# Convolution and input projection of a four-layer selective scan: from 128 output columns at once to pairs of 64

## The chip, the cores and the metric

The kernel runs on one core of one Trainium2 chip. The metric is the device time of one launch in microseconds; lower is better. A state in this text is one of the 16 state channels of the scan, and "128*64" in a row of the profile is a matmul with 128 rows of contraction and 64 output columns (output partitions).

## What is computed

Four layers are applied to x of 8 x 48 x 48 x 96, each as `x = x + ss2d(groupnorm(x))`. Cut to what matters, one layer is:

```
xz = x @ in_proj_w.T;  xc, z = split(xz)               # 192 channels each
xc = silu(depthwise_conv3x3(xc) + conv_b)              # over 48 x 48
for each of 4 directions k (rows, columns, both reversed):
    dt, B, C = split(x_proj[k] @ xc)                   # rank 6 or 16, 16, 16
    delta = softplus(dt_proj[k] @ dt + bias)
    h[n] = exp(delta*A[n]) * h[n] + delta*xc*B[n]      # a scan of 2304 steps, n = 0..15
    y += sum_n h[n]*C[n] + D*xc
out = out_proj @ (layernorm(y) * silu(z))
```

The last layer replaces the recurrence by a form with cumulative sums, of which the kernel computes 192 positions at each end and tests that the others have faded.

## The kernel before

Channels lie on partitions. Batches go in pairs, so a layer has four pairs, and the 192 channels of two batches make three tiles of 128 (t = 0 and 1 are the first 128 channels of one batch each, t = 2 the last 64 of both). In layers 0 to 2 the scan goes over 12 groups a pair (tile, phase, direction), each in three chunks of 768 positions, each chunk over 16 states: 4 x 3 x 12 x 3 x 16 = 6912 states in all.

One state takes these steps. SyncE fetches a row of C into `cb` and for 6 of 16 states a row of B into `bb` (`fetch`, L718). For the other 10, TensorE spreads B over the partitions into the PSUM tile `b` (`spread_rows`, L667, bf16, 96*64). ScalarE computes the decay `da` (L764), VectorE multiplies `b` by `du` (L794) and scans (L798), GpSimd multiplies by `bb` (L741) and by `cb` (L807), and TensorE adds pairs of states up into `acc` by the stationary matrix `twin` (`add_up`, L854, f32, 128*64 with 384 columns moving, a pair of halves). `prepare` makes the step sizes of the next chunk: L603, ScalarE's functions (L611 to L617), L623 (sums of four terms, again in pairs of 64 columns, both halves reading the same rows), copies to `dl` and `du` (L578).

The rest of a layer is written as generators whose steps go beside the scan. `prologue` of the next pair loads x, normalises it, projects it (L404 for the first 128 channels, L413 for the last 64, in row blocks of 480 or 384 positions) into the padded images `pad` and `pad2`, and convolves (`convolve`): for each of three tiles and five row blocks, nine matmuls L312 with diagonal stationary matrices `diag` add up in one PSUM bank, and ScalarE evicts them (L320). Then come the projections of x (L465) and the conversion of B to three bf16 parts. `epilogue` of the pair before does the layer norm (L1012 to L1018), the gate (L1074, L1078) and the output (L1092 to L1098, in the last layer L1113 to L1115).

```
            def beside():
                step(coming)

                for _ in range(10 if l in short else 0 if ends else 1):
                    side_step(rest) or side_step(behind, ahead)
```

So in layers 0 to 2 at most one side step goes with a state, and one matmul of the convolution is one step. In the last layer up to ten steps go with four states of the short form (class `Edge`, L930 to L995), and the convolution's matmuls stand in runs. PSUM banks for all of this are taken in turn from `psum` with two buffers (`bank()`).

For layers 0 to 2 `keep_order` holds every engine to the order in which the code issues instructions; the start and the last layer are ordered by the scheduler of the layer below.

Of the kernel before, what the change touches and what calls it, by code (L numbers as in the profile page):

```python
# [49 lines left out]
P = 128  # L50
NB, H, W, DM = 8, 48, 48, 96
# [52 lines left out]
def ss2d_layers_kernel(ctx: ExitStack, tc: tile.TileContext, x_in, consts, weights, out):  # L104
    nc = tc.nc
# [162 lines left out]
    def silu(o, i, **kw):  # L268

        with tc.issue_after(nc.scalar.activation(o, i, AF.Silu, **kw).ins):  # L270
            nc.scalar.preload_act_table_set("natural_log_exp_and_others")

    def bank():
        return psum.tile([P, BANK], F32, name="ps", tag="ps")
# [8 lines left out]


    GATED, READY = "gated", "ready"

    def prologue(l, p, short=False, first=False):
        ly = layers[l]
# [7 lines left out]
        def padded(name):  # L296
            pad = tmp.tile([P, H + 2, W + 2], F32, name=name, tag="tmp")
            nc.gpsimd.memset(pad[:, 0 : H + 2 : H + 1, :], 0.0)
            nc.gpsimd.memset(pad[:, 1 : H + 1, 0 : W + 2 : W + 1], 0.0)
            return pad  # L300

        def convolve(pad, t):

            while place["tiles"] < t and not first:
                yield GATED
            u[t] = upool.tile([P, L], F32, name=f"u_{l}_{p}_{t}", tag="u")
            for c0, m in CHUNKS:
                r0, nr = c0 // W, m // W
                ps = bank()
                for j in range(9):  # L310
                    dy, dx = divmod(j, 3)
                    nc.tensor.matmul(  # L312
                        ps[:, :m],
                        ly.diag[:, int(t == 2), j, :],
                        pad[:, r0 + dy : r0 + dy + nr, dx : dx + W],
                        start=(j == 0),
                        stop=(j == 8),
                    )
                    yield True
                nc.scalar.activation(  # L320
                    u[t][:, c0 : c0 + m], ps[:, :m], AF.Identity, bias=ly.column(t, C_CONVB)
                )
                yield
            silu(u[t], u[t])
            yield
# [6 lines left out]
        for b in range(2):  # L332
            x = tmp.tile([DM, L], F32, name=f"x_{l}_{p}_{b}", tag="tmp")
            if l == 0:
                loaded = []

                def load(c0, m):
                    ld = sm2.tile([P, 4, DM], F32, name="ld", tag="ld")
                    nc.sync.dma_start(
                        ld[: m // 4],  # L340
                        x_in[2 * p + b, c0 : c0 + m, :].rearrange("(q j) c -> q j c", j=4),
                    )
                    loaded.append(ld)

                load(*CHUNKS[0])
                load(*CHUNKS[1])
                for _ in range(3):
                    yield
                for i, (c0, m) in enumerate(CHUNKS):
                    q, ld = m // 4, loaded[i]  # L350
                    ps = bank()
                    for j in range(4):
                        nc.tensor.transpose(
                            ps[0:DM, j * q : (j + 1) * q], ld[:q, j, :], ident[:q, :q]
                        )
                    yield True
                    nc.scalar.copy(
                        x[:, c0 : c0 + m].rearrange("c (q j) -> c j q", j=4),
                        ps[0:DM, :m].rearrange("c (j q) -> c j q", j=4),
                    )  # L360
                    if i + 2 < NCH:
                        load(*CHUNKS[i + 2])
                    yield
                nc.sync.dma_start(src[b], x)
            else:
                nc.sync.dma_start(x, src[b])
            for _ in range(4):
                yield


            st = sm1.tile([DM, NCH, 6], F32, name="st", tag="st")
            for i, (c0, m) in enumerate(CHUNKS):
                nc.vector.bn_stats(st[:, i, :], x[:, c0 : c0 + m])
                if i % 2 == 1:
                    yield
            mv = sm1.tile([DM, 2], F32, name="mv", tag="mv")
            nc.vector.bn_aggr(mv, st.rearrange("p a b -> p (a b)"))
            yield
            ps = bank()
            nc.tensor.matmul(ps[0:DM, 0:1], minus_group, mv[:, 0:1], start=True, stop=True)  # L380
            yield True
            mg = sm1.tile([DM, 1], F32, name="mg", tag="mg")
            nc.scalar.copy(mg, ps[0:DM, 0:1])
            dv = sm1.tile([DM, 1], F32, name="dv", tag="dv")
            nc.scalar.activation(dv, mv[:, 0:1], AF.Square, bias=mg)
            nc.scalar.activation(dv, dv, AF.Identity, bias=mv[:, 1:2])
            yield
            ps = bank()
            nc.tensor.matmul(ps[0:DM, 0:1], group_w, dv, start=True, stop=True)
            yield True  # L390
            scale, shift = gn[:, b, 0:1], gn[:, b, 1:2]
            nc.scalar.activation(scale, ps[0:DM, 0:1], AF.Ln, bias=gn_eps[0:DM])
            nc.scalar.activation(scale, scale, AF.Exp, scale=-0.5)
            nc.scalar.activation(shift, mg, AF.Copy, scale=scale)
            nc.scalar.activation(x, x, AF.Identity, bias=shift, scale=scale)
            yield

            pad = padded(f"pad_{l}_{p}_{b}")
            q0 = 64 * b
            for c0, m in CHUNKS:  # L400
                r0, nr = c0 // W, m // W
                rows = slice(1 + r0, 1 + r0 + nr)
                ps = bank()
                nc.tensor.matmul(  # L404
                    ps[:, :m], ly.inw[:, 0:P], x[:, c0 : c0 + m], start=True, stop=True
                )
                yield True
                nc.scalar.copy(
                    pad[:, rows, 1 : W + 1], ps[:, :m].rearrange("p (r w) -> p r w", w=W)
                )  # L410
                yield
                ps = bank()
                nc.tensor.matmul(  # L413
                    ps[q0 : q0 + 64, :m], ly.inw[:, P:DIN], x[:, c0 : c0 + m], start=True, stop=True
                )
                yield True
                nc.scalar.copy(
                    pad2[q0 : q0 + 64, rows, 1 : W + 1],
                    ps[q0 : q0 + 64, :m].rearrange("p (r w) -> p r w", w=W),
                )  # L420
                yield
            if not (first and b == 1):
                yield from convolve(pad, b)
        yield from convolve(pad2, 2)


# [124 lines left out]
        if first:  # L551

            yield from x_projections((0, 0))
            yield READY
            yield from x_projections((1, 0))
            yield from convolve(pad, 1)
            yield from x_projections((0, 1), (1, 1))
        else:
            yield from x_projections((0, 0), (0, 1), (1, 0), (1, 1))
# [610 lines left out]
    def run(pairs, short):  # L1170
# [16 lines left out]
        def begin(l, p, first=False):  # L1187
            if l not in layers:
                layers[l] = Layer(l)
            return prologue(l, p, l in short, first)  # L1190
# [110 lines left out]
    ps = bank()  # L1301
# [100 lines left out]
```

## Time and profile before

| | |
|---|---|
| median of 3 runs | 20514.42 us (20494.02 to 20516.52) |
| profiled execution | 20509.65 us, its span 20507.7 us |
| mean granted TensorE clock | 0.904 |
| L312 matmul records, busy | 4320 (two for each of 2160 f32 matmuls), 2165.7 us |
| L404 matmul records | 320 |
| layers 0 to 2, from the first state to the last | 204 to 18564 us |
| last layer with its epilogues | 18564 to 20508 us |

The profile is of one execution. PE is TensorE's matmuls, PEld its weight loads, DVE VectorE, ACT ScalarE, POOL GpSimd, SP SyncE. Starts of matmuls are recorded and their ends are modelled, so the text takes the time from one start to the next where it says how long a matmul holds TensorE. A row of a group gives its count, then busy time and mean duration in ns, then the idle time ahead of it and what ended that. A row of the waits gives the total in us, the number of waits and the longest. `clock` is the share of full speed that TensorE was granted.

### The profile page before, as it was taken

How to read it: one execution, taken by the hardware profiler on the slowest of the kernel's cores; microseconds unless marked ns; L12 is line 12 of the kernel's file. 1: busy time of each engine (PE TensorE's matmuls, PEld its weight loads, DVE VectorE, ACT ScalarE, POOL GpSimd, SP SyncE). 2: the span in 40 equal slices, each digit the busy share in tenths (PEclk: the TensorE clock that was granted, in tenths of full speed). 3: DMA queues.
4: the chain of work that ended last, by engine and by line, in shares of the span. 5: the costliest groups of instructions: out<-in, count | busy, mean ns of one | idle time of the engine just before them, and what ended most of it. 6: DMA issues, size and time to landing. Idle time of an engine off the chain costs nothing. (4 is left out here: it accounts for less than half of the span.)

```text
span 20507.7 us, 304889 instructions
## 1 busy us (share of the span) xinstructions
PE 17283.2 (84%) x88322; PEld 7546.6 (37%) x88322; DVE 17656.0 (86%) x14161; ACT 16243.7 (79%) x30020; POOL 17768.2 (87%) x10121
## 2 busy tenths in 40 slices
PE   8888888888888888888888888888888888888886
PEld 2323333333333333333333333333333333335565
DVE  5999999999999999999999999989989989995543
ACT  5777887887887887887877887877877877877776
POOL 5999999999999999999999999999999999995432
PEclk8998998998998999998998999988988998999997
DMA  5888888888888888888888888888888888883221
GB/s 147 223 221 222 219 220 224 222 219 221 220 225 222 219 229 221 221 229 219 221 228 220 217 225 219 218 218 220 217 219 219 220 219 222 219 220 109 76 72 51
DMA packets 1963444, 4200.13 MB, mean 205 GB/s; under 512 B 369456, under 2 KB 720048, under 8 KB 1948592
## 3 DMA queue, kind: packets, MB, share of 16 engines
q1 hardware_dynamic: 1961776, 4180.52, 77.8%
q8 instruction: 726, 11.89, 0.3%
q14 instruction: 942, 7.72, 0.2%
HBM read 4026.64 MB, written 152.27 MB: 204 GB/s over the span
## 5 line engine op out<-in xcount | busy, mean ns | idle before, releaser
L807 POOL TENSOR_TENSOR cb<-cb,da 128x768 f32<-128x768 f32 x4320 | 7831.3, 1817 | 799.5 <-issue 258.3
L854 PE MATMUL acc<-cb,twin 128*64 128x384 f32 x27648 | 7018.1, 542 | 663.6 <-POOL cb L807 660.3
L798 DVE TENSOR_TENSOR_SCAN da<-da,carry,b 128x768 f32<-128x768 f32 x2880 | 5223.3, 1814 | 176.4 <-ACT b L764 2.3
L741 POOL TENSOR_TENSOR bb<-bb,du 128x768 f32<-128x768 f32 x2592 | 4714.0, 1819 | 361.0 <-DMA bb<-xd 207.8
L794 DVE TENSOR_TENSOR b<-du,b 128x768 f32<-128x768 f32 x4320 | 4087.6, 946 | 883.9 <-PE b L667 785.4
L807 POOL TENSOR_TENSOR cb<-cb,bb 128x768 f32<-128x768 f32 x2592 | 4705.1, 1815 | 155.0 <-DVE bb L798 57.1
L667 PE MATMUL b<-brow,pick 96*64 96x512 bf16 (+2 forms) x18816 | 2761.6, 355 | 1787.6 <-DVE da L798 1408.4
L764 ACT ACTIVATE da<-dl,a 128x768 f32<-128x768 f32 x4320 | 4013.6, 931 | 245.8 <-POOL cb L807 214.0
L854 PEld LDWEIGHTS acc<-cb,twin 128*64 128x64 f32 x27648 | 2268.9, 150 | 3089.4 <-issue 1400.3
L798 DVE TENSOR_TENSOR_SCAN bb<-b,carry,bb 128x768 f32<-128x768 f32 x1728 | 3109.0, 1799 | 114.8 <-ACT b L764 53.5
L764 ACT ACTIVATE b<-dl,a 128x768 f32<-128x768 f32 x2592 | 2334.4, 901 | 590.2 <-DVE da L798 558.4
L798 DVE TENSOR_TENSOR_SCAN da<-da,b 128x768 f32<-128x768 f32 x1440 | 2525.4, 1754 | 85.6 <-DVE b L794 0.9
L667 PEld LDWEIGHTS <-pick 96*64 96x64 bf16 x18816 | 974.1, 114 | 4192.1 <-DVE da L798 2506.3
L578 ACT COPY dl<-ps 64x384 f32<-64x384 f32 x3456 | 1635.3, 473 | 756.7 <-PE ps L623 720.7
L312 PE MATMUL ps<-pad,diag 128*128 128x480 f32 (+1 forms) x4320 | 2165.7, 599 | 11.5 <-DVE eyc L1087 9.9
L623 PE MATMUL ps<-du,cst 128*64 128x384 f32 (+1 forms) x7296 | 1709.7, 516 | 93.1 <-ACT du L617 77.0
L578 ACT COPY du<-ps 64x384 f32<-64x384 f32 x3456 | 1635.7, 473 | 190.0 <-DVE ps L634 91.2
L798 DVE TENSOR_TENSOR_SCAN bb<-b,bb 128x768 f32<-128x768 f32 x864 | 1502.2, 1739 | 94.9 <-ACT b L764 40.5
L623 PE MATMUL ps<-dl,cst 128*64 128x384 f32 (+1 forms) x7296 | 1412.4, 483 | 0.0
L312 PEld LDWEIGHTS ps<-pad,diag 128*128 128x128 f32 x4320 | 687.5, 191 | 1211.4 <-issue 1090.1
L603 PE MATMUL ps<-dts,w 6*128 6x384 f32 (+5 forms) x2432 | 946.3, 595 | 176.1 <-DMA dts<-xd 103.7
L611 ACT ACTIVATE du<-ps,w 128x384 f32<-128x384 f32 (+1 forms) x912 | 521.4, 572 | 622.3 <-PE ps L603 611.5
(144 smaller groups left out, 19159.8 us busy)
## 6 DMA issues: line engine op xcount, KB each, us to landing
cb<-xd SPq DMA_DIRECT2D x13952, 192.0 KB
bb<-xd SPq DMA_DIRECT2D x5184, 192.0 KB
brow<-xb SPq DMA_DIRECT2D x864, 72.0 KB
yd<-y SPq DMA_DIRECT2D x48, 1152.0 KB
ey<-yd SPq DMA_DIRECT2D x256, 216.0 KB
cb<-xd SPq DMA_DIRECT2D x128, 384.0 KB
ex<-xs SPq DMA_DIRECT2D x256, 108.0 KB
xd<-xt SPq DMA_DIRECT2D x32, 684.0 KB
```

Of the source, the lines that this page charges most:

```text
L312: nc.tensor.matmul(ps[:, :m], ly.diag[:, int(t == 2), j, :], pad[:, r0 + dy : r0 + dy + nr, dx : dx + W], start=(j == 0), stop=(j == 8),)
L578: nc.scalar.copy(z[64 * h : 64 * h + 64, g, at], v[64 * g : 64 * g + 64])
L603: nc.tensor.matmul(o[:, :m], ly.dtw[q0 : q0 + r, k, chans], dts[q0 : q0 + r, at], start=True, stop=True,)
L611: nc.scalar.activation(e, v, AF.Abs, bias=bias)
L623: nc.tensor.matmul(v[half], ident[:, half], z1, start=(i == 0), stop=(i == 3))
L667: nc.tensor.matmul(o[64 * h : 64 * h + 64], pick[:, b, n : n + 1].to_broadcast([2 * NR, 64]), rows, start=True, stop=True,)
L741: nc.gpsimd.tensor_mul(b, b, self.du[n % 2])
L764: nc.scalar.activation(da, self.dl[n % 2], AF.Exp, scale=layers[self.l].a2[:, int(self.t == 2), n % 2, k, i : i + 1],)
L794: nc.vector.tensor_mul(b, self.du[n % 2], b)
L798: nc.vector.tensor_tensor_scan(way(h), way(da), way(b), start, ALU.mult, ALU.add)
L807: nc.gpsimd.tensor_mul(c, c, h)
L854: nc.tensor.matmul(self.acc[64 * g : 64 * g + 64, a, : self.m // 2], twin, c[:, a, :], start=False, stop=(pair + 2 == NS and not self.turns),)
```

## The change

Each convolution matmul and each input projection to the first 128 channels is issued as two matmuls, one for columns 0 to 63 of the stationary matrix into partitions 0 to 63 of the same PSUM bank and one for columns 64 to 127 into partitions 64 to 127. Both read the same moving rows. The steps at which the generators yield are the same. Everything else, L413 with its 64 columns included, stays. Below the change, line numbers are higher by one to three.

```diff
     GATED, READY = "gated", "ready"
+    halves_of = [slice(64 * g, 64 * g + 64) for g in range(2)]
...
                 for j in range(9):
                     dy, dx = divmod(j, 3)
-                    nc.tensor.matmul(
-                        ps[:, :m],
-                        ly.diag[:, int(t == 2), j, :],
-                        pad[:, r0 + dy : r0 + dy + nr, dx : dx + W],
-                        start=(j == 0),
-                        stop=(j == 8),
-                    )
+                    for half in halves_of:
+                        nc.tensor.matmul(
+                            ps[half, :m],
+                            ly.diag[:, int(t == 2), j, half],
+                            pad[:, r0 + dy : r0 + dy + nr, dx : dx + W],
+                            start=(j == 0),
+                            stop=(j == 8),
+                        )
                     yield True
...
                 ps = bank()
-                nc.tensor.matmul(
-                    ps[:, :m], ly.inw[:, 0:P], x[:, c0 : c0 + m], start=True, stop=True
-                )
+                for half in halves_of:
+                    nc.tensor.matmul(
+                        ps[half, :m], ly.inw[:, half], x[:, c0 : c0 + m], start=True, stop=True
+                    )
                 yield True
```

## The prediction

> **What bounds the kernel now.** I read the busy row first, then the slices, the sums over stretches of time, the waits of VectorE and GpSimd, and last the timeline of TensorE around one convolution matmul.
>
> ```profile
> PE 17283.2 (84%) x88322; PEld 7546.6 (37%) x88322; DVE 17656.0 (86%) x14161; ACT 16243.7 (79%) x30020; POOL 17768.2 (87%) x10121
> ...
> PEclk8998998998998999998998999988988998999997
> ```
>
> Four engines lie between 79% and 87%, so the average decides nothing. In the stretch from 200 to 18564 us (the 6912 states of layers 0 to 2, by the count of L807) and inside it in the 66 stretches that hold convolution matmuls (each from the first to the last L312 of a burst), the answers over windows end with these lines; then come two whole chunks of 16 states, one with 13 convolution matmuls and one with none.
>
> ```profile
> 200.00:18564.00 18364.00, 15553.88 (x78072) 6350.09 (x78070) 16765.45 (x12610) 14739.91 (x27238) 17058.32 (x9682) 0.91 0.85 221
> ...
> sum 5716.21, PE 5336.45 PEld 1947.55 DVE 5380.45 ACT 4479.37 POOL 5466.59; mean PE 80.86 PEld 29.51 DVE 81.52 ACT 67.87 POOL 82.83
> ...
> 7381.30:7421.20 39.90, 38.37 (x179) 12.90 (x178) 38.14 (x29) 31.39 (x64) 39.12 (x24) 1.00 0.90 229
> 7757.80:7796.80 39.00, 27.26 (x140) 12.88 (x138) 37.01 (x27) 28.46 (x57) 39.00 (x23) 0.81 0.87 227
> ```
>
> Columns: length, busy PE, PEld, DVE, ACT, POOL, granted clock, DMA share, GB/s. GpSimd is the fullest engine: 93% over the main stretch, 96% inside the convolution stretches. The reader is to see the last two rows: 16 states take 39.90 us with TensorE at 96%, and 39.00 us with TensorE at 70% and GpSimd at 100%. Taking a third of TensorE's work away is worth 0.9 us in 40. The floor is GpSimd's own work: (4320 x 1.817 + 2592 x (1.819 + 1.815)) / 6912 = 2.50 us a state from the rows of L807 and L741, where the convolution stretches run at 2.55 (5716.21 us over their 2240 states).
>
> TensorE still has a say, through lateness:
>
> ```profile
> DVE b L794 <- PE b L667: 785.4, 745, 5.9
> ...
> POOL cb L807 <- PE acc L854: 83.5, 75, 2.4
> ```
>
> **What the Trainium skill says.** (1) "TensorEngine Tiling (Array Packing)", Key Properties: changing the tiling mode, not just the tile, drains TensorE. The timeline agrees:
>
> ```profile
> 5013.72 1.46 PE L623 MATMUL ps<-du,cst 128*64 128x384 f32 x8
> 5015.01 0.49 PE L667 MATMUL b<-brow,pick 96*64 96x512 bf16 x4
> ...
> 5034.37 0.81 PE L854 MATMUL acc<-cb,twin 128*64 128x384 f32 x4
> 5035.02 1.46 PE L623 MATMUL ps<-dl,cst 128*64 128x384 f32 x8
> 5036.40 1.07 PE L312 MATMUL ps<-pad,diag 128*128 128x480 f32 x2
> 5037.40 0.52 PE L667 MATMUL b<-brow,pick 96*64 96x512 bf16 x4
> 5037.75 0.81 PE L854 MATMUL acc<-cb,twin 128*64 128x384 f32 x4
> 5038.49 1.07 PE L312 MATMUL ps<-pad,diag 128*128 128x480 f32 x2
> ```
>
> Take start to next start. L623 holds TensorE for 1.29 us when a 64-column matmul follows and 1.38 when L312 follows; L854 for 0.65 and 0.74. So going to 128 columns costs 0.09 us before L312 begins. (2) "TensorE: Matmul & The Clock Gate", Part 3, says that matmuls in different column groups run concurrently. L623 agrees: its two halves read the same rows, as the new pairs will, and eight records (four matmuls, two records for each f32 matmul) take 1.29 us, so a pair of 384 columns takes 0.645 us. (3) The same page, Part 1: a TensorE that idles is throttled to half clock until it has been busy again. The two chunks agree: granted clock 1.00 with TensorE at 96%, 0.81 with it at 70%.
>
> **The change part by part.**
>
> *Slot of a convolution matmul.* Now: 1.00 us (5036.40 to 5037.40) plus 0.09 ahead of it. After: a pair of 480 columns, 0.645 x 480/384 = 0.81 us, with no switch as its neighbours have 64 columns too. The saving is 0.28 us; a little comes from what follows (L667's first records stand 0.24 us apart after L312, 0.22 otherwise), so 0.30. The short row blocks (384 columns, 0.84 us now) save the same.
>
> *How many.* Following TensorE's records in order from 200 to 18564 us, 1665 convolution matmuls and 120 input projections (L404) stand there; 1623 have 64-column work on both sides, 162 follow a 128-column matmul of the epilogue. 1623 x 0.30 + 162 x 0.10 (the switch only moves) = about 500 us of TensorE time, 2.7% of the main stretch.
>
> *How much of it is on the path.* Nearly all of it lies beside GpSimd and VectorE. The convolution holds one PSUM bank over nine side steps that are dealt out one per state, so a shorter slot does not bring the next step forward; it only lets L667, L854, L623 and L603 behind it start sooner. What can come back is at most GpSimd's idle time in those stretches: 5716.2 - 5466.6 = 250 us. By the inferred releasers some 60 us of it waited for TensorE directly (41 for L854, 20 for L667 and L603), another 125 is put down to "issue", VectorE's scans and ScalarE, which themselves wait for TensorE part of the time (VectorE's idle time there is 238 us, 187 of it for L667), and the rest is DMA. I take 60 us plus a quarter of the 125, about 90 us gained.
>
> *What is given back.* TensorE's idle share in these stretches grows from 7% to about 15%. Stretches elsewhere with such a load (chunks whose full-clock demand is 81 to 87%) show the half clock for about 10% of the time, against 3.4% in the convolution stretches now. GpSimd idles 9 points more while the clock is halved (8.8 to 13.6% against 4 to 6.5%, from its gaps set against the clock record). 5716 x 0.066 x 0.09 = 34 us. The sign of that cause is unsure, since idling also brings the half clock on; bounds 0 and 110 (the 25% half clock of the rest of the main stretch: 5716 x 0.215 x 0.09).
>
> *Weight loads.* Four loads of 64 columns replace two of 128. PEld's row of L312 has 191 ns, that of L854 150 ns: 0.60 us in a slot of 0.81, still beside the streaming, as in L623's pairs. Cost nothing; were that cover gone, up to 0.2 us for each slot would be back and the change would be near nothing.
>
> *ScalarE's evictions (L320, L408)* keep their number and shape and wait for both halves. No DMA is added or moved; in the built program the queues of SP, GpSimd, ScalarE and VectorE keep their order through layers 0 to 2. A few instructions of layer 3 change places.
>
> *The start.* Up to 46 us the input projections alternate with L413 at half clock on the only path: 1.90 us for L404, 1.79 for L413. After: 1.61 each (0.81 doubled), 0.47 us less for each of ten alternations: 5 us gained. The two dense runs of 45 convolution matmuls (36.5 us each, 0.81 us a matmul) already stream at the pairs' rate: nothing.
>
> *Layer 3 (18564 to the end).* TensorE is busiest there (1583 of 1944 us), but 405 matmuls stand in runs of up to 9 and more, at 0.403 us a record, again the pairs' rate. Only run ends matter, and some neighbours there (L969, L1012) have 128 columns, which puts switches in where none were: between -10 and +10 us. The exchanged places I bound at 1% of the stretch, 20 us either way, and take 0.
>
> *Sum.* 90 - 34 + 5 = about 60 us less than the profiled execution's 20509.65 us (span 20507.7): 20450. The median of the runs is 20514.42, 5 us higher, which moves nothing.
>
> **The rivals.**
>
> 1. *Hidden.* GpSimd and VectorE set the pace, and each stall that TensorE no longer makes is ended a moment later by DMA, ScalarE or the scan. For it: the 0.9 us in 40 between the two chunks, and GpSimd's waits for DMA. Against it: 187 us of VectorE's idle time there ends on L667. Time 20470 to 20555.
>
> 2. *The clock takes it back (slower).* TensorE falls idle often enough to lose its clock inside the convolution stretches. L667's burst, 0.33 us at full clock, doubles, and VectorE and then GpSimd wait for it. For it: outside these stretches the clock is halved for a quarter of the time and VectorE's idle share is 8.5% against 4.2%; chunks with nothing but 9 convolution matmuls beside their states take 2.6 us a state, those with 13, at full clock throughout, 2.49. Against it: the chunk at 0.81 lost nothing, as TensorE ran ahead there. Price: 110 us at the rest's clock share, less about 50 gained, so +60, 20570. It decides from a half-clock share of some 20%.
>
> 3. *The pairs do not overlap,* or their moving rows (runs of 48 of a padded 50) stream more slowly twice at once. Two single halves in turn take 1.61 us, +0.5 us x 1665 = +850 us of work on a TensorE with 380 us of room: at least +450. L623 speaks against it; 3 in 100.
>
> 4. *The whole idle time comes back:* -250 us, 20260. The DMA share of 0.88 and more in these stretches speaks against it.
>
> **How the numbers follow.** A measurement here tells about 0.2%, 41 us, from no change. My forecast (20330 to 20473) and rival 4 get 0.55, rival 1 gets 0.25, rivals 2 and 3 together 0.20. The predicted time is 20450. The range 20330 to 20560 takes in two thirds of the ceiling of 250 with the start, and on the other side the bounds of the clock and of layer 3's order; rivals 3, 4 and the far half of rival 2 stay out. The likeliest case's own range is 20330 to 20473.
>
> **What would show it.** The new matmul row should read 128*64 128x480 x8640 with 0.81 us from its four records to the next work, and L854 ahead of it 0.65: else the slot is wrong. TensorE's busy sum over the convolution stretches should fall by some 300 to 500 us and GpSimd's share rise from 95.6 towards 97%; if it does not rise, rival 1. VectorE's wait for L667 should fall from 785 us; if it rises together with a granted clock under 0.90, rival 2. A gain that lies in layer 3 or the start, or any change of more than 250 us in the main stretch, would make this prediction wrong.

## The result and the profile after

| | before | after |
|---|---|---|
| median, 7 runs each | 20505.76 us | 20422.49 us (20407.38 to 20450.3) |
| ratio | | 0.9959, interval 0.9949 to 0.9968 |
| profiled execution | 20509.65 us | 20422.49 us |
| its span | 20507.7 us | 20420.1 us |
| up to the first state's L807 (after: L810) | 206.8 us | 189.9 us |
| layers 0 to 2, first to last state | 18357.4 us | 18291.8 us |
| the rest | 1943.5 us | 1938.4 us |

The changed kernel is 0.41% faster, 83 us by the medians. The last three rows come from one execution of each kernel; they are read from the starts and ends of that line's instructions and split the 88 us between the two profiled spans: 17 in the start, 66 in layers 0 to 2, 5 in layer 3. The busy row and the granted clock of the page after:

```profile
PE 16937.8 (83%) x92962; PEld 7830.6 (38%) x92962; DVE 17652.1 (86%) x14161; ACT 16233.2 (79%) x30020; POOL 17769.0 (87%) x10121
...
PEclk8988998898998998999988898988998988989997
```

TensorE has 4640 more matmul records (two for each of 2160 + 160 further matmuls) and is 345 us less busy. The other engines have the same work to within 11 us. The timeline of TensorE in a convolution stretch of the changed kernel (columns: start, length with the modelled end, instructions):

```profile
5021.77 0.81 PE L857 MATMUL acc<-cb,twin 128*64 128x384 f32 x4
5022.41 0.97 PE L314 MATMUL ps<-pad,diag 128*64 128x480 f32 x4
5023.22 0.49 PE L670 MATMUL b<-brow,pick 96*64 96x512 bf16 x4
5023.55 0.81 PE L857 MATMUL acc<-cb,twin 128*64 128x384 f32 x4
5024.19 0.97 PE L314 MATMUL ps<-pad,diag 128*64 128x480 f32 x4
```

From start to next start: L857 holds TensorE for 0.64 us, L314 for 0.81. The slot came out as predicted, and not here alone: of the slots that stand by themselves at full clock with 480 columns, the median is 1.00 us before (1303 slots) and 0.81 after (931). Below are windows of the changed kernel: layers 0 to 2, the sum over its convolution stretches, and the same two whole chunks as those shown of before.

```profile
190.00:18482.00 18292.00, 15228.81 (x81640) 6675.07 (x81640) 16755.43 (x12608) 14723.97 (x27228) 17057.18 (x9682) 0.90 0.85 222
...
sum 5606.46, PE 5002.31 PEld 2227.45 DVE 5322.71 ACT 4418.02 POOL 5401.72; mean PE 73.56 PEld 32.76 DVE 78.28 ACT 64.97 POOL 79.44
...
7327.60:7366.80 39.20, 34.69 (x204) 15.54 (x204) 38.08 (x29) 31.36 (x64) 39.05 (x23) 1.00 0.87 228
7707.80:7746.90 39.10, 27.52 (x140) 10.33 (x138) 37.37 (x27) 28.84 (x58) 39.08 (x23) 0.81 0.87 226
```

Over layers 0 to 2 TensorE is 325 us less busy (15553.88 to 15228.81), with the same work on GpSimd. The clock hides more of the saving: at half clock a matmul takes twice as long (the two records of an L416 start 0.80 us apart at half clock in the start, 0.40 at full clock). With the busy time at half clock halved, TensorE has 467 us less (14047 to 13580). In the convolution stretches GpSimd's share goes from 95.6% to 96.3%. (The two sums of these stretches should be compared by their shares: the changed kernel's stretches hold 65 us less work of GpSimd, so the 334 us between their TensorE times are not all a saving.)

The chunk with 13 convolution matmuls took 39.90 us and takes 39.20; the one without any took 39.00 and takes 39.10. Neither pair is typical. The 16 chunks with 13 convolution matmuls went from 39.9 to 39.5 us on average, and the chunk without any is the shortest of its kind: the 239 chunks in which no convolution matmul stands take 43.4 us on average, since other work stands in them. VectorE and GpSimd wait less for TensorE over layers 0 to 2, but only a little:

```profile
DVE b L797 <- PE b L670: 713.1, 619, 6.0
...
POOL cb L810 <- PE acc L857: 60.7, 57, 2.8
```

785.4 and 83.5 us before. Much of the time that TensorE no longer spends went into its own waits: it is idle for 604 us of the convolution stretches instead of 380 (length less busy time in the sums shown), most of that until VectorE's scan has let go of a buffer (313 us, before 229) or GpSimd has made `cb` (218, before 97).

### The profile page after: what moved, and what is told of

The parts are those of the page before. It is cut to its first block, busy times and chain, and to the rows that moved or that the text cites. A ratio compares the mean times of both kernels' runs of the same rounds, so it can differ in the third digit from the quotient of the medians.

```text
span 20420.1 us, 314181 instructions
## 1 busy us (share of the span) xinstructions
PE 16937.8 (83%) x92962; PEld 7830.6 (38%) x92962; DVE 17652.1 (86%) x14161; ACT 16233.2 (79%) x30020; POOL 17769.0 (87%) x10121
## 5 line engine op out<-in xcount | busy, mean ns | idle before, releaser
L810 POOL TENSOR_TENSOR cb<-cb,da 128x768 f32<-128x768 f32 x4320 | 7834.1, 1818 | 741.0 <-issue 249.7
L857 PE MATMUL acc<-cb,twin 128*64 128x384 f32 x27648 | 7282.8, 544 | 805.7 <-POOL cb L810 801.3
L810 POOL TENSOR_TENSOR cb<-cb,bb 128x768 f32<-128x768 f32 x2592 | 4707.4, 1816 | 142.6 <-DVE bb L801 54.3
L670 PE MATMUL b<-brow,pick 96*64 96x512 bf16 (+2 forms) x18816 | 2900.2, 355 | 1894.8 <-DVE da L801 1523.7
L857 PEld LDWEIGHTS acc<-cb,twin 128*64 128x64 f32 x27648 | 2454.6, 151 | 3127.7 <-POOL cb L810 1425.5
L670 PEld LDWEIGHTS <-pick 96*64 96x64 bf16 x18816 | 1111.6, 116 | 4156.3 <-DVE da L801 2662.4
L314 PE MATMUL ps<-pad,diag 128*64 128x480 f32 (+1 forms) x8640 | 2300.2, 570 | 21.1 <-DVE eyc L1090 9.0
L626 PE MATMUL ps<-du,cst 128*64 128x384 f32 (+1 forms) x7296 | 1761.7, 521 | 83.1 <-ACT du L620 67.8
L626 PE MATMUL ps<-dl,cst 128*64 128x384 f32 (+1 forms) x7296 | 1482.1, 482 | 0.0
L314 PEld LDWEIGHTS ps<-pad,diag 128*64 128x64 f32 x8640 | 727.8, 140 | 889.1 <-issue 751.1
```

The source lines that it names most:

```text
L314: nc.tensor.matmul(ps[half, :m], ly.diag[:, int(t == 2), j, half], pad[:, r0 + dy : r0 + dy + nr, dx : dx + W], start=(j == 0), stop=(j == 8),
L626: nc.tensor.matmul(v[half], ident[:, half], z1, start=(i == 0), stop=(i == 3))
L670: nc.tensor.matmul(o[64 * h : 64 * h + 64], pick[:, b, n : n + 1].to_broadcast([2 * NR, 64]), rows, start=True, stop=True,)
L810: nc.gpsimd.tensor_mul(c, c, h)
L857: nc.tensor.matmul(self.acc[64 * g : 64 * g + 64, a, : self.m // 2], twin, c[:, a, :], start=False, stop=(pair + 2 == NS and not self.turns),)
```

## The experiments

The times of the stages, in us, come from the one profiled execution of each kernel; the ratio is from all its runs, against runs of the kernel before on the same chip.

| kernel | ratio (interval) | start | layers 0 to 2 | rest |
|---|---|---|---|---|
| before | | 206.8 | 18357.4 | 1943.5 |
| changed | 0.9959 (0.9949 to 0.9968) | 189.9 | 18291.8 | 1938.4 |
| conv_only | 0.9979 (0.9972 to 0.9986) | 207.4 | 18317.9 | 1945.6 |
| inproj_only | 0.9979 (0.9973 to 0.9986) | 187.4 | 18330.3 | 1937.0 |
| conv_fill | 1.0053 (1.0039 to 1.0066) | 217.1 | 18338.1 | 2037.8 |
| two_taps | 0.9869 (0.9854 to 0.9884) | 136.3 | 18266.6 | 1826.9 |
| conv_double | 1.0094 (1.0078 to 1.0109) | 185.8 | 18561.1 | 1938.3 |
| warm_before | 0.9989 (0.9980 to 0.9997) | 186.8 | 18339.1 | 1941.9 |
| state_fill | 0.9991 (0.9983 to 1.0000) | 190.0 | 18359.5 | 1940.9 |
| wide_epi | 0.9943 (0.9929 to 0.9956) | 183.7 | 18272.2 | 1935.3 |
| wide_edge | 0.9968 (0.9956 to 0.9981) | 182.9 | 18282.1 | 1939.2 |
| best | 0.9944 (0.9930 to 0.9957) | 186.3 | 18252.7 | 1932.7 |

How far single executions scatter can be read from kernels with the same code in a stage. In layers 0 to 2 warm_before is the kernel before, and takes 18 us less; wide_edge is the changed kernel, and takes 10 us less. So a difference of some 20 us in that column tells nothing by itself. The diffs are cut to the lines that matter; in conv_fill, conv_double and state_fill, `zeros` is a tile of 128 x 64 zeros.

**conv_only and inproj_only: the two halves of the change.** The first keeps L404 as it was, the second keeps L312.

```diff
-                for half in halves_of:
-                    nc.tensor.matmul(
-                        ps[half, :m], ly.inw[:, half], x[:, c0 : c0 + m], start=True, stop=True
-                    )
+                nc.tensor.matmul(
+                    ps[:, :m], ly.inw[:, 0:P], x[:, c0 : c0 + m], start=True, stop=True
+                )
```

> Only the convolution in pairs of 64, the input projection with 128 columns as before. The changed kernel gained 17 us up to the first state, 66 us in layers 0 to 2 and 6 us after. Theory: the start's 17 us come from the clock, which the input projections without switches raise 16 us earlier, so they belong to the input projection; the rest belongs to the convolution. Expected: 55 to 75 us less than before (ratio 0.9963 to 0.9973), first state at 203 to 207 us. Rival (the pairs of the convolution alone make the start quicker): first state near 190 us and the whole 83 us.

> Only the input projection in pairs of 64, the convolution as before. Theory: first state at 190 to 194 us, with the clock at full speed some 16 us earlier than before; in layers 0 to 2 120 slots become 0.3 us shorter, which is beside GpSimd's work, so 0 to 15 us. Expected 12 to 30 us less than before (0.9985 to 0.9994). Rival: the start gains only the 5 us of the shorter slots.

Each half is 0.21% faster than before, and together they make the whole. 2160 convolution matmuls bring as much as 160 input projections. The start belongs to the projection alone (187.4 us against 207.4), as the theory said; but both totals miss the expected ones: the convolution brings less (about 42 us by the ratio, not 55 to 75), the projection more (about 42, not 12 to 30). To see where in layers 0 to 2, I took the difference to the kernel before chunk by chunk, 16 states each, and summed it over 102 chunks with 9 or more convolution matmuls and over 70 with input projections in them:

```
                 conv chunks    projection chunks
conv_only           -38 us            -4 us
inproj_only          -7              -18
changed             -32              -16
warm_before          -6               -2
```

One chunk differs by about 1 us from run to run, so a sum over 100 scatters by some 10 us; warm_before, whose code is the same there, shows it. Within that, each half acts where it stands. Of the changed kernel's 66 us, 17 lie in neither kind of chunk, and 10 of warm_before's 18 do too. 1665 slots shortened by 0.30 us brought about 40 us (8%). The 120 projections, some 36 us of TensorE time, brought about 17, with an uncertainty of 8 or so, so between a quarter and two thirds. Why a slot of the projection seems to be worth more was not tried.

**conv_fill: TensorE's time put back without the switches.** Zeros are added to the sums by a pair of 64 columns, in the start and layer 3 too.

```diff
+                    if 0 < j < 8:
+                        for half in halves_of:
+                            nc.tensor.matmul(
+                                ps[half, :224], zeros, pad.rearrange("p r w -> p (r w)")[:, 0:224],
+                                start=False, stop=False,
+                            )
```

> The changed kernel plus, after seven of nine convolution steps, a pair of 64 columns with 224 moving columns and a stationary matrix of zeros, added to the same bank (adds nothing to the sums). It puts back about 0.29 us of TensorE time for each convolution step (0.37 us, seven of nine), what the pairs saved, without the switches between 64 and 128 columns. Theory (the gain in layers 0 to 2 is TensorE's shorter time and nothing else of the switch): layers 0 to 2 lose the 66 us again within 25, the start keeps 10 to 17 us, so 10 to 35 us less than before in all. Rival (the drains at the switches hurt in themselves, the time does not matter): it stays 60 to 85 us under before. Rival (the clock: a busier TensorE keeps its full clock): faster than the changed kernel, 90 us or more under before.

The total misses the expectation, 0.53% slower than before, because the expectation forgot that the filler also stands in the start (+27 us against the changed kernel; 90 x 0.29 = 26) and in layer 3 (+99 us; 405 x 0.29 = 117), where the convolution runs without anything to hide it. Where the question was asked it answers: layers 0 to 2 lose 46 us and stand 19 under before, about where warm_before stands (18 under) without any change there. The chunks tell more: the convolution's gain is gone (-1 us) and the projection's is kept (-19). So the convolution's gain is TensorE's time; another effect of the drain, if there is one, is smaller than the 10 us or so by which these sums scatter. More work for TensorE brought the half clock in these stretches back to 3.9% of the time (before 3.4, changed 7.4), and no net gain came of it.

**two_taps and conv_double: less and more TensorE work.** two_taps leaves out seven of the nine taps, so its result is not the convolution's.

```diff
two_taps
-                    for half in halves_of:
+                    for half in halves_of if j in (0, 8) else ():
conv_double
+                    if 0 < j < 8 and l < NLAYER - 1 and not first:
+                        for half in halves_of:
+                            nc.tensor.matmul(
+                                ps[half, :m], zeros, pad.rearrange("p r w -> p (r w)")[:, 0:480][:, :m],
+                                start=False, stop=False,
+                            )
```

> The changed kernel with only the first and last of the nine taps computed (seven matmul pairs of each nine are left out; the steps are the same). TensorE loses another 7/9 of 0.81 us for each convolution step, about 1050 us in layers 0 to 2. Theory (GpSimd's floor): GpSimd has 213 us of idle time left in the convolution stretches, a good part of it DMA and ScalarE, so layers 0 to 2 gain at most 100 us more; in the start 2 x 27 us and in layer 3 up to 405 x 0.63 = 255 us go away directly. Expected 250 to 420 us under the changed kernel, with layers 0 to 2 between 0 and 100 us of that. Rival (TensorE is the bound in these stretches): layers 0 to 2 gain more than 200 us. Rival (clock): layers 0 to 2 become slower than in the changed kernel, since TensorE idles and stays at half clock.

> The changed kernel plus, in layers 0 to 2 alone, after seven of nine convolution steps a second pair of 64 columns of the same length with zeros as stationary matrix (adds nothing to the sums). 0.78 x 7/9 = 0.61 us more for each of 1665 steps, 1010 us of TensorE work, where the changed kernel has 609 us of TensorE idle time in the convolution stretches. Theory (TensorE's time is nearly free until its idle time is used up, then it counts in full): layers 0 to 2 take 400 to 500 us more than in the changed kernel, which is 330 to 430 more than before. Rival (every microsecond counts at the 8% of the gain): 80 us more than in the changed kernel. Rival (it counts in full from the start): 1000 us more.

The sums over the convolution stretches, first two_taps, then conv_double:

```profile
sum 5679.35, PE 4542.97 PEld 1962.68 DVE 5401.34 ACT 4494.51 POOL 5482.94; mean PE 70.98 PEld 30.67 DVE 84.40 ACT 70.23 POOL 85.67
```

```profile
sum 6055.93, PE 5723.28 PEld 2545.47 DVE 5492.07 ACT 4561.29 POOL 5604.82; mean PE 90.85 PEld 40.40 DVE 87.18 ACT 72.40 POOL 88.97
```

Both expectations sized the work a little too high. The long row blocks have slots of 0.81 us and the short ones of 0.64, so a mean slot is 0.77 us. two_taps leaves out 1295 pairs in layers 0 to 2, 1000 us. conv_double has 1155 pairs more, 900 us and not 1010: the condition `l < NLAYER - 1 and not first` also leaves out the first pair, a third of whose convolution stands beside layer 0, and layer 3's first pair, which stands beside layer 2.

Taking another 1000 us of TensorE work away brought layers 0 to 2 only 25 us: GpSimd stays at 96.5% of these stretches. That is inside the expectation for them; the whole came out short of it (190 us under the changed kernel, by the ratios 185) because layer 3 gave 112 us for up to 255. Adding 900 us cost 269, where the theory said 400 to 500 and the rival 80. With the right count the theory's rule gives about 300 (900 less the idle time of 604), but TensorE ends at 94.5% busy, so it did not use up all its idle time. With the points between them, the time of layers 0 to 2 against TensorE's work is a bent line (changes of work worked out from the slots):

```
from              to              TensorE work   layers 0 to 2    rate
two_taps          changed             +1000 us       +25 us         3%
changed           conv_fill            +480          +46           10%
conv_fill         conv_double          +420         +223           53%
```

The bend to the last row is clear; the first two rates differ by little more than the scatter of 20 us. The change lies on the flat part. In two_taps the half clock has 25% of the time in the convolution stretches (7.4% in the changed kernel), and GpSimd idles 4.3% of the half-clock time there against 3.2% of the rest: with this little to do, TensorE's half clock costs almost nothing.

**warm_before: the start and the clock.** Four unused matmuls while TensorE waits. The edit stands in the loop over the two batches of the first pair, so that both batches got it, not the first alone as the expectation says. That is why the start became shorter by 20 us where 6 to 10 were expected; the whole is 0.11% faster than before.

```diff
             nc.tensor.matmul(ps[0:DM, 0:1], group_w, dv, start=True, stop=True)
+            if first:
+                spare = bank()
+                for _ in range(4):
+                    nc.tensor.matmul(spare[:, : 2 * P + DM], ident, cst, start=True, stop=True)
             yield True
```

> The kernel before, with four extra matmuls of 128 columns (352 moving columns, result unused) once, in the start, in the 4.3 us in which TensorE waits for the first normalised x ahead of the first input projection. Theory (the start's 17 us are the clock's): TensorE is busy from 24 us on, the full clock comes by about 31 us instead of 48.9, the first batch's input projections (17.8 us from 28.2 to 46.0) take 10 to 12 us, and its convolution ends some 8 us earlier; the second batch has no extra work and keeps its 17.8 us. First state at 197 to 201 us against 206.8, the whole 5 to 10 us less than before. Rival (the drains of the switches and the slots alone): first state at 206 to 208 us.

The first input projections in the timelines of the kernel before, of the changed one, and of warm_before:

```profile
28.21 1.97 PE L404 MATMUL ps<-x,w 96*128 96x480 f32 x2 [4.36 <-ACT x L395]
30.11 1.86 PE L413 MATMUL ps<-x,w 96*64 96x480 f32 x2
31.90 1.97 PE L404 MATMUL ps<-x,w 96*128 96x480 f32 x2
```

```profile
28.60 1.87 PE L407 MATMUL ps<-x,w 96*64 96x480 f32 x4 [4.47 <-ACT x L397]
30.26 1.81 PE L416 MATMUL ps<-x,w 96*64 96x480 f32 x2
31.14 2.21 PE L407 MATMUL ps<-x,w 96*64 96x480 f32 x4
33.18 0.97 PE L416 MATMUL ps<-x,w 96*64 96x480 f32 x2
34.02 1.03 PE L407 MATMUL ps<-x,w 96*64 96x480 f32 x4
```

```profile
29.69 1.07 PE L408 MATMUL ps<-x,w 96*128 96x480 f32 x2
30.69 1.02 PE L417 MATMUL ps<-x,w 96*64 96x480 f32 x2
31.64 1.07 PE L408 MATMUL ps<-x,w 96*128 96x480 f32 x2
```

Before, L404 to L413 takes 1.90 us, and all ten projections of the batch go at that pace. In the changed kernel it begins at 1.66 and is 0.85 from 34 us on. In warm_before the old matmuls of 128 columns take 1.00. The record of the granted clock says why: full clock from 48.9 us before, from 32.9 us in the changed kernel, from 29.4 us in warm_before. So an earlier full clock alone, with the switches in place, is enough for a gain like the start's: warm_before has its first state at 186.8 us. The changed kernel gets the full clock 16 us earlier than before, and so does inproj_only (33.5 us), while conv_only (49.7 us) does not; what sets them apart between 28 and 33 us is that the projections come in pairs and no longer switch.

The clock is not the whole of the changed kernel's 17 us, though. These are the times from the first projection of a batch to its convolution, for both batches:

| kernel | projections | clock in them | us |
|---|---|---|---|
| before | 128 and 64 columns | half | 17.8, 17.8 |
| changed | 64 columns | half, then full | 10.3, 11.3 |
| warm_before | 128 and 64 columns | full | 9.4, 9.4 |
| best (below) | 64 columns | full | 8.3, 8.3 |

The projections save 14 of the 17 us, the two convolutions, which no longer begin at half clock, the other 3. While the changed kernel was still at half clock, an alternation took 2.5 to 3.1 us (from L407 to the next L407: 28.60 to 31.14, 91.18 to 93.77 and 93.77 to 96.90) against 3.7 before. By that estimate, ten alternations at half clock would have brought 5 to 11 us without any help of the clock.

**state_fill: is the half clock of the other stretches worth anything?**

```diff
+                if n < NS - 1 and not place["conv"]:
+                    nc.tensor.matmul(
+                        self.acc[64 * g : 64 * g + 64, a, :192], zeros, c[:, a, :192],
+                        start=False, stop=False,
+                    )
```

> The changed kernel plus, for 15 of 16 states of layers 0 to 2 and only while no convolution is under way, a pair of 64 columns with 192 moving columns and zeros as stationary matrix into the sums of the states (adds nothing): 0.32 us more TensorE work for a state, no switch. In the stretches without convolution the half clock has 26% of the time now. Theory (the clock costs there: GpSimd idles 13% in half-clock time and 6.7% else): the half clock falls to 10 to 15%, and layers 0 to 2 gain 50 to 100 us against the changed kernel. Rival (TensorE's time counts as it did for the input projection, a third to a half of each microsecond): about 4500 states x 0.30 us = 1350 us more work cost more than 200 us. Rival (GpSimd's floor hides it): within 40 us of the changed kernel.

Outside the convolution the half clock fell from 25.8% to 14.1% of the time, as the theory said. Layers 0 to 2 became 68 us slower, neither a gain nor over 200. So a lower share of half clock did not pay for the work that bought it, some 1200 us (3665 pairs at about 0.33 us). What a full clock would be worth without that work is not shown; that the half clock follows TensorE's idling more than it causes GpSimd's is a reading that fits, not one that this run proves.

**wide_epi, wide_edge, best: the same edit elsewhere.** More of the 128-column matmuls in pairs: the epilogue's (the layer norm's below, the gate's L1074 in the same form), the last layer's sums (L969) in the same form; best is wide_epi with the unused matmuls of warm_before, in pairs.

```diff
-                    nc.tensor.matmul(ps[:, t, :], own, z[:, t, :], start=True, stop=False)
-                    nc.tensor.matmul(ps[:, t, :], off_2[:, t, :], z[:, 2, :], start=False, stop=True)
+                    for o in halves_of:
+                        nc.tensor.matmul(ps[o, t, :], own[:, o], z[:, t, :], start=True, stop=False)
+                    for o in halves_of:
+                        nc.tensor.matmul(ps[o, t, :], off_2[:, t, o], z[:, 2, :], start=False, stop=True)
```

> The changed kernel with the matmuls of the epilogue that have 128 columns (the layer norm's two, and the gate's) in pairs of 64 as well; those with 96 columns stay. For each of 192 row groups in layers 0 to 2 three visits to 128 columns go away, about 0.3 us each: 170 us of TensorE time, nearly all outside the convolution stretches. At the rate of the convolution (40 us for 500) 14 us, at the rate of the input projection (17 us for 36) 80 us. Expected 14 to 80 us under the changed kernel. Rival (GpSimd's floor): within 15 us of it.

> The changed kernel with the sums of the last layer's short form (128 columns, 192 moving) in pairs of 64: 768 matmuls in runs of one to four, some 250 visits to 128 columns at 0.3 us each, 75 us of TensorE time in a stretch in which TensorE is the fullest engine (1579 of 1938 us). Theory (TensorE is on the path there): 25 to 75 us under the changed kernel, all after the last state of layers 0 to 2. Rival (ScalarE's chain sets the pace there): within 15 us; the same if a matmul of 128 columns follows anyway.

> The changed kernel with the epilogue's matmuls of 128 columns in pairs of 64 as well and, in the start, four unused pairs of 64 columns (352 moving columns) in TensorE's wait ahead of the input projection of each of the first pair's two batches. From the runs before: the epilogue some 20 us in layers 0 to 2, the start 5 to 10 us (first state at 180 us, where the changed kernel has 190). Expected 20370 to 20400 us, ratio 0.993 to 0.995 to the kernel before. Rival (the start's clock has nothing left to give once the projections are in pairs): as with the epilogue alone, 20390 us.

wide_epi has a median of 20389.59 us, 33 under the changed kernel: inside the expectation, at the lower rate. All five of its runs (20375 to 20396 us) lie under the fastest of the changed kernel's seven (20407), though the intervals of the two ratios overlap. By the profile 20 of the 33 us are in layers 0 to 2, which is the scatter of that column. wide_edge brought nothing to layer 3 (1939.2 us against 1938.4), as its rival has it, though TensorE is the fullest engine there; what sets the pace there was not tried.

best has a median of 20374.54 us, but its ratio, 0.9944, is that of wide_epi (the runs of the kernel before beside it were 10 us faster), so the unused matmuls brought nothing to the whole that shows. Its start, 186.3 us, misses the expected 180 and is no shorter than that of wide_epi (183.7) or wide_edge (182.9), whose code up to the first state is the changed kernel's (189.9). The trace shows why. The unused matmuls did their work: the second convolution ends at 133.7 us, against 137.4 in wide_epi and in the changed kernel. But from there to the first state best takes 52.6 us, the changed kernel 52.5 and wide_epi 46.2. In wide_epi the full clock lasts until 151.2 us, in best until 138.5 and in the changed kernel until 142.1. So the rival, that nothing was left to gain, is not shown: 4 us were gained and then lost in a stretch whose clock differs between runs of the same code, by up to 7 us of start.

## Why the prediction was right, and which terms were not

Forecast: 60 us less than the profiled execution, 20450, with faster as the likeliest. Measured: 88 us less by the profiled span, 83 by the medians.

*The slot* was right: 0.81 us, and 0.64 for L857 ahead of it. *Weight loads* stay hidden: 136 ns a load (the median of the 8640 loads of L314), four in a slot. *TensorE's time* was right too: 467 us less over layers 0 to 2 at full clock, for a forecast of 500. 325 us of it show as less busy time; the rest went into more half-clock time.

*How much is on the path* was the wrong step, in two ways. The convolution was to bring 90 us before the clock's share and 56 after it; conv_only shows about 40 after it, and so less than 50 before it. All 60 us that GpSimd spent waiting for TensorE in these stretches were counted as won; the waits for L854, L667 and L603 went from 61 to 38 us (41.2 to 16.5, 10.5 to 8.5, 9.1 to 12.5). And the 120 input projections of layers 0 to 2 got no share of the gain, since it was read from the convolution stretches alone; they bring about 17 us in their chunks. The two chunks of which the prediction says that a third of TensorE's work is worth 0.9 us in 40 are no measure of this either: the one without convolution is the shortest of 239.

*What the clock takes back* was sized at 34 us and is smaller. The half clock in the convolution stretches rose to 7.4%, not 10%, since TensorE's idle share grew to 10.8%, not 15%. GpSimd idles 6.9% of that time and 3.4% of the rest, not nine points more, so 5606 x 0.040 x 0.035 = 8 us by the same working. The nine points were not in the trace of before either: it has 9.7% against 4.2% in these stretches and 13.7% against 6.5% outside them, five to seven points. And the half clock need not be the cause of that idling: in two_taps, with 25% half clock, the difference is one point.

*The start* was sized at 5 us from slots at half clock and gave 17. Two things were left out. The projections in pairs reach the full clock within their batch, where those before stayed at half clock throughout. And L416 (L413 before), with 64 columns and no switch around it, holds the next L407 back for 0.88 us at half clock (30.26 to 31.14), not the 1.61 that the prediction took. The prediction had named a gain in the start as a sign against itself; a fifth of the gain lies there.

*Layer 3*: 5 us of gain, inside its -10 to +10.

So layers 0 to 2, forecast at 56 and measured at 66, came out near by luck: errors that offset each other, measured in one execution that scatters by 20 us. Most of what the total missed is the start.

The rivals: *hidden* is what most of the 500 us met; its GpSimd floor shows in two_taps. *The clock takes it back* did not happen: the half clock stayed far under the 20% from which it was to decide, and two_taps, at 25% with TensorE at 80%, is not slower than the changed kernel. *Pairs that do not overlap* is excluded by the slot: 0.81 us, where two halves in turn were to take 1.61. Of *the whole idle time* of GpSimd in these stretches, 250 us by the sum shown of before, 205 are left.

## What to carry to other kernels

Where one engine is at 96% of a stretch and another at 93%, taking a tenth of the second's work away was worth 8% of what was taken here, and taking a fifth more away some 3%. Adding work cost 10% of it at first and about half of it once the second engine was nearly full. So read the gain from the idle time of the fullest engine, and only from the part that waits on the engine you relieve, and do not count all of that part.

A visit to another array shape cost about 0.3 us of TensorE time among the scan's matmuls. Where nothing covers it, it counts: at full clock the five visits of a batch in the start took 1.1 us more than pairs did (9.4 against 8.3), 0.2 us each. There ten projections brought 17 us with the clock's help, where 1665 convolution matmuls in a covered loop brought 40. Put the sum of a change together stage by stage and run its halves apart, since a right total can hide two wrong terms; and before reading a stage's difference of 20 us, look at two executions with the same code in it.

## What the runs showed of the hardware that I had not expected

Alternating between 128 and 64 columns kept the clock down. In the kernel before, TensorE had work all the time from 28.2 to 46.0 us and stayed at half clock until 48.9 us; the second batch (99.6 to 117.4, full clock at 120.6) and both batches of conv_only show the same. In the eight kernels that have the projections in 64 columns throughout and nothing ahead of them, the full clock came at 32.9 to 35.2 us. With 4.9 us of matmuls ahead of it (warm_before) the full clock came at 29.4 us, and the same alternation then ran at full clock to its end. That it is the drains at the switches which hold the clock down is the likely reading; nothing else than the column count was varied.

Less half clock did not help where TensorE is covered, at least not when it was bought with work: 11.7 points less of it outside the convolution, for some 1200 us more work, went with 68 us more in layers 0 to 2.
